# Four graph layers on one core: 64-column products in blocks of 24, a price for fp32 weight loads in the planner, a row's wide product last, and a second strip buffer

## The chip, the core and the metric

The kernel runs on one core of a Trainium2 chip. The engines that matter here are TensorE (PE in the profile; its weight loads are listed apart as PEld), VectorE (DVE), ScalarE (ACT), GpSimd (POOL) and SyncE (SP), which issues nearly all DMAs. The metric is device time in microseconds, the median over the runs; lower is better.

## The reference

There are 16 independent graphs of 1024 nodes with 128 features. Each graph has an adjacency matrix of 1024 x 1024 floats, of which some 1.5% are not zero and whose pattern is symmetric. Four layers follow each other. Each takes h = relu(layernorm(x)) and adds its result to x:

```
layer 0   z = adj^T h / degree ; relu([h, z] W^T + b)
layer 1   leaky_relu((adj h / degree) W^T + b)
layer 2   twice: s[n, m] = sigmoid(relu(a[n] + b[m] + be1) . we2 + be2), a = x Wa, b = x Wb
                 messages = (adj * s) x ; two dense products on [x, messages] ; layernorm
layer 3   e = leaky(wh1[n] + wh2[m]) on the edges ; softmax over m ; attention times Wh ; elu
```

Layer 2 is the costly one. The score s needs a 128-wide hidden vector for every pair of nodes, and only pairs with an edge matter.

## The kernel before

**Edges instead of pairs.** The nodes of a graph are cut into 8 tiles of 128. A bucket is a pair of tiles (t, u); there are 28 off the diagonal and 8 on it. `count` and `build` find, for every bucket, the edges in it and make one-hot fp8 matrices: `st` and `om` bring node features to edge slots (up to 320 slots off the diagonal, 480 on it), `onT` and `omT` bring scores from slots back to a 128 x 128 block. Buckets are handled in 9 groups of four: a diagonal group, seven groups off the diagonal, a diagonal group.

**A round** (`round`, one for each of the two sublayers of layer 2) walks over the 9 groups. For each bucket and direction, `gather` makes a row `pre` in PSUM: two products with `om` moving (320 or 480 columns, L1345) and two with `st` moving (176 or 240 columns, L1351), all added into one bank. The stationary operands are the node features: their fp16 high and low parts, `parts` and a copy of them with swapped halves, `both`, which a DMA makes. ACT (L1366) and DVE (L1367) turn the row into two fp16 parts of `hid`. `dots` multiplies `hid` by a sign column in products of one column each (L1391), ACT applies tanh (L1412), and `scores` spreads the scores with one DVE multiplication of 1024 elements for each direction (`val`, L1443). `scatter` (L1488) adds them into a bank `p`, of which there is one: the first direction with full 128-column output, the second direction (d = 1) with products that write 64 of the 128 output partitions each, 6 for a bucket and 24 for a group. These are the rows `128*64` in the profile, called 64-column products here after the columns of the array that they use. DVE then multiplies the bank by the adjacency block (`upd`, L1495), and `messages` (L441) multiplies by the features in fp32.

**Three lanes.** `weave` generates the work of three lanes side by side: `main` of batch b (lane m, the two rounds), `last` of batch b-1 (lane c: the second update of layer 2 and layer 3) and `first` and `build` of batch b+1 (lane a: layers 0 and 1, then the one-hot matrices). Lanes a and c consist mostly of fp32 products. Layer 3 in lane c walks over strips of the transposed adjacency: a strip is fetched by a DMA on SP's queue (L1579), three DVE operations and one ACT operation work on it (`e`, L767 to L773), and PE multiplies (`hp`, L441). The strips lie in a tile with the tag `strip`, which has one buffer. Layer normalization (`spread`) puts its statistics into a tile `bn`, which has two.

**The planned order.** The order in which the lanes were generated isn't the order of issue. When all operations are recorded, `Issue` lists them with the engine, an estimated duration (`costs`) and the tiles that they use, and plans one order for each engine's queue. `walk` goes through the operations in the order of time: on each queue it takes, of those that are ready, the one with the highest rank. Ranks come from a walk backward from the end; `order` repeats this in four passes and keeps the plan that ends first; `settle` ties the operations of each engine into the planned order, SP's DMA issues included. On PE the walk adds a price when one product follows another of a different form, and the form is narrow or not:

```python
    def switched(self, j, was, back):
        one, two = (self.form[j], was) if back else (was, self.form[j])
        return 0.0 if one == two else NARROW_NS if two else WIDE_NS
```

with 94 ns into the narrow form and 119 ns out of it. The estimated duration of a narrow product is 29 ns, of other fp16 or fp8 products n / 2.4 + 2.5 ns, and an fp32 product counts two passes of at least 112 ns. Nothing is added for a weight load that the product before it is too short to hide. The 24 narrow products of a group are 24 separate entries for the planner.

Of the kernel before, what the change touches and what calls it, by code (L numbers as in the profile page):

```python
# [10 lines left out]
F32 = mybir.dt.float32  # L11
# [48 lines left out]
RESULT_NS = {"PE": 163.0, "Activation": 120.0, "DVE": 88.0, "Pool": 80.0}  # L60
NARROW_NS, WIDE_NS, HELD_NS = 94.0, 119.0, 130.0
DMA_NS, DMA_NS_PER_BYTE, DMA_NS_BEHIND, DMAS = 1900.0, 3.9e-3, 3.3e-3, 8
PASSES = 4


class Issue:
# [3 lines left out]
    def __init__(self, tc, ops, fixed):  # L70
        self.tc, self.ops, self.fixed = tc, ops, fixed
        self.tiles = {t.name: t for t in tc.tiles}
        self.queue = [str(i.engine).split(".")[-1] for i in ops]
        self.kind = [type(i).__name__.removeprefix("Inst") for i in ops]
        self.links()
        self.costs()

    def span(self, arg):
# [51 lines left out]
    def costs(self):  # L130
# [3 lines left out]
        for op, queue, kind in zip(self.ops, self.queue, self.kind):  # L134
            out, form = op.outs[0].bass_ap, False
# [3 lines left out]
            if kind == "Matmult":  # L139
                n = self.size(op.ins[0])  # L140
                form = out.shape[0] < 128
                if op.ins[0].dtype == F32:
                    busy = max(n / 1.2 + 6, 112) * (1 if op.is_transpose else 2)
                else:
                    busy = 29 if form else max(n / 2.4 + 2.5, 25)
            elif kind == "DMACopy":
                size = n * WIDTH[op.outs[0].dtype] * out.shape[0]
                inside = all(a.space == bass.MemoryType.SB for a in (out, aps[0]))
                busy = 630 if inside else 470
                late = DMA_NS + size * DMA_NS_PER_BYTE - busy  # L150
            elif queue == "Activation":
                busy = n / 1.2 + (50 if psum else 92) + 92 * (len(aps) - 1)
            elif queue == "DVE":
                wide = [a for a in aps if a.size() > 128]
                fast = kind == "TensorScalarPtr" and len(wide) == 1 and not psum
                if kind in ("BNStats", "TensorReduce"):
                    n = self.size(op.ins[0])
                busy = n * (0.53 if fast else 1.0625) + 55 + 64 * (len(aps) - len(wide))
                rows = {v[1] for v in map(self.span, (*op.ins[:1], *op.outs[:1])) if v}
                busy += HELD_NS * (len(rows) > 1)  # L160
            else:
                busy = 1560
            self.bytes.append(size)
            self.busy.append(busy)
            self.late.append(busy + late)
            self.form.append(form)

    def joined(self):
# [23 lines left out]
    def switched(self, j, was, back):  # L192
        one, two = (self.form[j], was) if back else (was, self.form[j])
        return 0.0 if one == two else NARROW_NS if two else WIDE_NS

    def walk(self, rank, seq, back=False):
# [8 lines left out]
        soon, now = {q: [] for q in queues}, {q: [] for q in queues}  # L205
        free, sent, was = dict.fromkeys(queues, 0.0), [(0.0, 0.0, 0)] * DMAS, False

# [22 lines left out]
        for _ in range(n):  # L230
# [4 lines left out]
            while soon[q] and soon[q][0][0] <= at:  # L235
                heappush(now[q], heappop(soon[q])[1:])
            j = heappop(now[q])[1]
            more = 0.0
# [6 lines left out]
            elif q == "PE":  # L245
                at += self.switched(j, was, back)
                was = self.form[j]
            start[j], free[q] = at, at + self.busy[j]
# [52 lines left out]
def tile_four_gnn_layers(  # L301
# [142 lines left out]
    class Layers:  # L444
# [22 lines left out]
        def small(self, shape, tag, name):  # L467
            return self.work.tile(shape, F32, tag=f"{tag}{self.lane}", name=name)

# [329 lines left out]
    class Edges:  # L799
# [115 lines left out]
        def scale_terms(self):  # L915
# [15 lines left out]
            for l in range(L):  # L931
                for h in range(2):
# [3 lines left out]
                    )  # L936
            bnd = work.tile([P, L], F32, tag="end", name="bnd")
            nc.vector.tensor_reduce(
# [47 lines left out]
        def strip(self, name):  # L986

            if self.rows_of.get("c"):
                return flat(self.row("c", name))
            return self.work.tile([P, 2 * 3 * P], F32, tag="strip", name=name, bufs=1)  # L990

# [79 lines left out]
        def count(self, s, has, name):  # L1071
# [12 lines left out]
            s.wid = self.work.tile([P, nb], F32, tag="wid", name=f"wid_{name}")  # L1084
            end = self.work.tile([P, nb], F32, tag="end", name=f"end_{name}")
            nc.vector.tensor_scalar(s.wid, s.cnt, -1.0, None, op0=OP.add)
# [203 lines left out]
        class Group:  # L1290
# [43 lines left out]
            def gather(self, i):  # L1334
# [5 lines left out]
                for d in range(self.nd):  # L1340
                    pre = path.m.one(f"pre_{self.name}_{i}_{d}")

                    parts, _ = path.parts[u // Q]
                    for k in range(2):
                        nc.tensor.matmul(  # L1345
                            pre[:, :c], parts[:, k, u % Q, 1 - d], om,
                            start=(k == 0), stop=True, skip_group_check=True,
                        )
                    _, both = path.parts[t // Q]
                    for k, (at, first) in enumerate(((0, 0), (c - n, back))):  # L1350
                        ins = nc.tensor.matmul(  # L1351
                            pre[:, at : at + n], both[:, k, t % Q, d], st[:, first : first + n],
                            start=False, stop=True, skip_group_check=True,
                        )
# [462 lines left out]
```

## Time and profile before

| | |
|---|---|
| median of 3 runs | 4661.11 us (4647.63 to 4667.04) |
| profiled execution | 4639.45 us, span 4637.7 us |
| granted TensorE clock, mean | 0.982 |
| PE | 4359.0 us, 94% of the span, 53685 products |
| weight loads (PEld) | 3581.9 us, 77% |
| DVE | 3873.0 us, 84% |
| ACT | 2992.3 us, 65% |
| POOL | 194.4 us, 4% |
| DMA | 603.41 MB, 130 GB/s on average |

The span runs from the first to the last instruction of one profiled execution. An fp32 product of the program appears as two passes in the records. Busy time of PE counts a product from its start to its end, and products overlap, so a row of the timeline such as `0.86 ... x24` gives the time from the first start to the last end of 24 products. The distance from one row's start to the next row's start tells how long PE needed. In the timeline a name such as `p<-omT,val` means the tile that is written and the tiles that are read, and `128*64 128x128` means 128 rows and 64 columns of the array with 128 elements moving for each partition. A batch takes some 280 to 290 us.

### The profile page before, as it was taken

The page shows a single profiled execution, that of the slowest core. Times are in us where ns is not written, and L with a number is a line of the kernel's source. Part 1 is how long each engine was busy: PE and PEld are TensorE (multiplying, and loading weights), DVE is VectorE, ACT ScalarE, POOL GpSimd, SP SyncE. Part 2 cuts the span into 40 slices and gives each one's busy share as a digit, 9 for nine tenths or more (in the row PEclk, how much of TensorE's full clock was granted, in tenths as well). Part 3 has the DMA queues.
Part 4 walks back from the last instruction along what each step waited for, and adds up shares of the span by engine and source line. Part 5 has one row for each costly group of instructions (what it writes and reads, how often), then busy time and mean ns, then how long its engine had stood idle before and what let it go on. Part 6 is the DMA issues. An engine that isn't in the chain of part 4 may idle for free.

```text
span 4637.7 us, 132212 instructions
## 1 busy us (share of the span) xinstructions
PE 4359.0 (94%) x53685; PEld 3581.9 (77%) x53685; DVE 3873.0 (84%) x9128; ACT 2992.3 (65%) x7238; POOL 194.4 (4%) x137
## 2 busy tenths in 40 slices
PE   6999999999999999999999999999999999999986
PEld 5787778777787777878878787777877777788765
DVE  4777797987979889797897979879797897979977
ACT  5666575675756767576675766757576675766643
POOL 0000100000000000000000000000000000000000
PEclk7999999999999999999999999999999999999997
DMA  7262635445363542635436353453634436344221
GB/s 213 66 198 68 196 94 164 114 127 162 90 185 100 147 142 83 196 107 147 126 94 198 89 162 115 130 165 85 189 103 140 142 83 196 107 145 123 80 80 57
DMA packets 852857, 603.41 MB, mean 130 GB/s; under 512 B 128528, under 2 KB 782608, under 8 KB 852240
## 3 DMA queue, kind: packets, MB, share of 16 engines
q1 hardware_dynamic: 847136, 593.24, 44.3%
q8 instruction: 423, 6.93, 0.6%
q10 hardware_dynamic: 5104, 1.65, 0.1%
q14 instruction: 194, 1.59, 0.1%
HBM read 446.44 MB, written 100.66 MB: 118 GB/s over the span
## 4 chain that ended last, share of the span: by engine, by line
PE 63%; DVE 21%; ACT 6%; DMA 6%; issue 2%; SPq 1%; POOL 1%; ACTq 0%; DVEq 0%; POOLq 0%
PE pre L1345 8%; PE nb L545 8%; PE p L1488 7%; PE msg L441 7%; PE sc L1391 5%; PE pre L1351 5%; DVE hid L1367 4%; PE h L599 4%; DVE val L1443 3%; PE hp L441 3%; PE bb L553 2%; PE xn L608 2%; PE tn L1040 2%; DMA at<-in_adj_dram 2%; DMA both<-part 2%
## 5 line engine op out<-in xcount | busy, mean ns | idle before, releaser
L1367 DVE SCALAR_TENSOR_TENSOR hid<-pre,hid 128x320 f16<-128x320 f32 (+1 forms) x2048 | 1004.1, 508 | 168.6 <-ACT hid L1366 157.9
L1366 ACT ACTIVATE hid<-pre 128x320 f16<-128x320 f32 (+1 forms) x2048 | 906.0, 461 | 330.0 <-PE pre L1351 301.4
L1345 PE MATMUL pre<-om,part 128*128 128x320 fp8e4 (+1 forms) x4096 | 970.9, 309 | 9.8 <-DVE hid L1367 3.7
L1351 PE MATMUL pre<-st,both 128*128 128x176 fp8e4 (+1 forms) x4096 | 681.5, 244 | 21.9 <-DMA both<-part 21.5
L1443 DVE TENSOR_TENSOR val<-onT,u 128x1024 f32<-128x1024 fp8e4 x576 | 695.5, 1218 | 1.6
L441 PE MATMUL msg<-upd,xf 128*128 128x128 f32 (+3 forms) x3008 | 638.7, 327 | 3.8 <-DVE upd L1495 3.8
L1351 PEld LDWEIGHTS <-both 128*128 128x128 f16 x4096 | 392.6, 98 | 180.1 <-issue 35.9
L1391 PE MATMUL sc<-slide,hid 128*128 128x1 f16 x12800 | 435.4, 163 | 28.5 <-DVE hid L1367 26.4
L1391 PEld LDWEIGHTS <-hid 128*128 128x128 f16 x12800 | 410.0, 96 | 53.4 <-DVE hid L1367 40.9
L441 PEld LDWEIGHTS msg<-upd,xf 128*128 128x128 f32 x3008 | 414.4, 191 | 27.6 <-DVE upd L1495 5.5
L1412 ACT ACTIVATE tan<-sc,be_s,down 128x8 f32<-128x8 f32 (+1 forms) x960 | 296.6, 358 | 193.8 <-PE sc L1391 189.1
L1495 DVE SCALAR_TENSOR_TENSOR upd<-p,adj 128x512 f32<-128x512 f32 x512 | 351.6, 687 | 72.4 <-PE p L1488 70.5
L1206 ACT ACTIVATE om<-pm 128x320 fp8e4<-128x320 f32 (+1 forms) x576 | 270.4, 469 | 206.7 <-PE pm L1152 200.0
L1488 PE MATMUL p<-val,omT 128*128 128x64 f16 (+1 forms) x6528 | 373.0, 204 | 27.9 <-DVE val L1443 26.9
L1345 PEld LDWEIGHTS <-part 128*128 128x128 f16 x4096 | 345.2, 98 | 69.0 <-issue 36.8
L1488 PEld LDWEIGHTS <-omT 128*128 128x128 fp8e4 x6528 | 329.3, 97 | 55.0 <-issue 45.4
L441 PE MATMUL hp<-wh,e 128*128 128x129 f32 x2048 | 328.7, 287 | 16.7 <-DVE e L773 16.6
L1191 ACT ACTIVATE onT<-pn 128x256 fp8e4<-128x256 f32 (+1 forms) x576 | 252.3, 438 | 68.1 <-PE pn L1137 62.5
L441 PEld LDWEIGHTS hp<-wh,e 128*128 128x128 f32 x2048 | 274.3, 195 | 26.8 <-DVE e L773 21.7
L1116 DVE TENSOR_SCALAR st<-far,wid 128x384 fp8e4<-128x384 f16 (+1 forms) x576 | 238.6, 428 | 59.4 <-PE pre L1351 37.8
L1112 ACT ACTIVATE far<-iota_off,mid 128x384 f16<-128x384 f16 x448 | 270.0, 625 | 17.3 <-DVE st L1116 14.7
L545 PEld LDWEIGHTS nb<-z,l 128*128 128x128 f32 x2048 | 254.8, 194 | 33.8 <-issue 19.3
(224 smaller groups left out, 7890.8 us busy)
## 6 DMA issues: line engine op xcount, KB each, us to landing
at<-in_adj_dram SPq DMA_DIRECT2D x128, 512.0 KB, 5.1
ct<-in_adj_dram SPq DMA_DIRECT2D x128, 512.0 KB, 5.4
adjT<-tn SPq DMA_DIRECT2D x128, 512.0 KB, 6.3
l<-adjT SPq DMA_DIRECT2D x128, 512.0 KB, 5.8
adj<-adjT SPq DMA_DIRECT2D x256, 256.0 KB, 3.5
a<-adjT SPq DMA_DIRECT2D x128, 384.0 KB, 3.8
both<-part SPq DMA_DIRECT2D x256, 128.0 KB, 3.4
adj<-adjT SPq DMA_DIRECT2D x448, 64.0 KB, 2.6
```

Source lines behind the costliest of these rows:

```text
L441: nc.tensor.matmul(dst, left, right, start=opened is None, stop=True, skip_group_check=True)
L545: nc.tensor.matmul(ps, mat[:, k], z[:, k], start=(k == 0), stop=(k == T - 1))
L1206: nc.scalar.activation(om, pm, AF.Copy, saturate=False)
L1345: nc.tensor.matmul(pre[:, :c], parts[:, k, u % Q, 1 - d], om, start=(k == 0), stop=True, skip_group_check=True,)
L1351: ins = nc.tensor.matmul(pre[:, at : at + n], both[:, k, t % Q, d], st[:, first : first + n], start=False, stop=True, skip_group_check=True,)
L1366: nc.scalar.activation(hid[:, 0, :c], pre[:, :c], AF.Relu)
L1367: nc.vector.scalar_tensor_tensor(hid[:, 1, :c], pre[:, :c], 0.0, hid[:, 0, :c], op0=OP.max, op1=OP.subtract)
L1391: nc.tensor.matmul(sc[:, k, g : g + 1], self.hid[self.done + g][:, v, at : at + P], sign, start=(g, v, k) == (*order[0], 0), stop=True, sk ...
L1412: nc.scalar.activation(dst, src, AF.Tanh, bias=path.be2[:, self.l : self.l + 1], scale=path.down[:, self.l : self.l + 1],)
L1443: nc.vector.tensor_tensor(val, onT[:, i : i + each].rearrange("p i (c n) -> p i c n", n=n), v.rearrange("p k i o -> p i k o").to_broadcast ...
L1488: nc.tensor.matmul(dst, left, right, start=n < first, stop=True, skip_group_check=True)
L1495: nc.vector.scalar_tensor_tensor(upd, ps, S_SCALE, self.adj[:, d * Q : (d + 1) * Q], op0=OP.add, op1=OP.mult,)
```

## The change

The planner gets four things. Products have one of three forms instead of two: narrow, full, and wide for fp32 ones. `switched` adds to the price of a change of form a price for an fp32 load behind a product of another form: what is missing from 108 ns in the duration of the product ahead. `blocks` finds runs of narrow products that write the same tile (the bank `p`), moves the needs of all of them to the first, and so makes one block of the 24. And `walk`, once PE is inside a block, goes on with that block as long as members of it are ready.

In `gather` the order of the four products of a row becomes `om`, `st`, `st`, `om`; only the first opens the accumulation, as before.

The strip of layer 3 gets two buffers instead of one. The tiles `bn`, `seen`, `end` and `bnd` get one buffer instead of two.

```diff
-NARROW_NS, WIDE_NS, HELD_NS = 94.0, 119.0, 130.0
+NARROW_NS, WIDE_NS, LOAD_NS, HELD_NS = 94.0, 119.0, 108.0, 130.0
...
             if kind == "Matmult":
                 n = self.size(op.ins[0])
-                form = out.shape[0] < 128
+                form = "narrow" if out.shape[0] < 128 else "full"
                 if op.ins[0].dtype == F32:
+                    form = "wide"
+
                     busy = max(n / 1.2 + 6, 112) * (1 if op.is_transpose else 2)
                 else:
-                    busy = 29 if form else max(n / 2.4 + 2.5, 25)
+                    busy = 29 if form == "narrow" else max(n / 2.4 + 2.5, 25)
...
+    def blocks(self):
+
+
+        line = [j for j in range(len(self.ops)) if self.queue[j] == "PE"]
+        self.block, run = {}, []
+        for j in (*line, None):
+            if j is not None and self.form[j] == "narrow" and (
+                not run or self.uses[j][-1] == self.uses[run[0]][-1]
+            ):
+                run.append(j)
+                continue
+            for k in run:
+                self.block[k] = run[0]
+                if k > run[0]:
+                    for i, done in self.needs[k].items():
+                        if i not in run:
+                            self.needs[run[0]][i] = self.needs[run[0]].get(i, False) or done
+            run = [j] if j is not None and self.form[j] == "narrow" else []
...
     def switched(self, j, was, back):
-        one, two = (self.form[j], was) if back else (was, self.form[j])
-        return 0.0 if one == two else NARROW_NS if two else WIDE_NS
+        if was is None:
+            return 0.0
+        k, i = (j, was) if back else (was, j)
+        one, two = self.form[k], self.form[i]
+        if one == two:
+            return 0.0
+        cost = NARROW_NS * (two == "narrow") + WIDE_NS * (one == "narrow")
+        return cost + max(0.0, LOAD_NS - self.busy[k]) * (two == "wide")
...
-            j = heappop(now[q])[1]
+            if q == "PE" and len(now[q]) > 1 and was in self.block:
+                best = min(now[q], key=lambda v: (self.block.get(v[1]) != self.block[was], v))
+                now[q].remove(best)
+                heapify(now[q])
+                j = best[1]
+            else:
+                j = heappop(now[q])[1]
...
                 at += self.switched(j, was, back)
-                was = self.form[j]
+                was = j
...
         def small(self, shape, tag, name):
-            return self.work.tile(shape, F32, tag=f"{tag}{self.lane}", name=name)
+            more = {"bufs": 1} if tag in ("bn", "seen") else {}
+            return self.work.tile(shape, F32, tag=f"{tag}{self.lane}", name=name, **more)
...
-            return self.work.tile([P, 2 * 3 * P], F32, tag="strip", name=name, bufs=1)
+            return self.work.tile([P, 2 * 3 * P], F32, tag="strip", name=name, bufs=2)
...
-            end = self.work.tile([P, nb], F32, tag="end", name=f"end_{name}")
+            end = self.work.tile([P, nb], F32, tag="end", name=f"end_{name}", bufs=1)
...
                     parts, _ = path.parts[u // Q]
-                    for k in range(2):
+                    _, both = path.parts[t // Q]
+                    terms = [
+                        (pre[:, at : at + n], both[:, k, t % Q, d], st[:, first : first + n])
+                        for k, (at, first) in enumerate(((0, 0), (c - n, back)))
+                    ]
+                    ends = [(pre[:, :c], parts[:, k, u % Q, 1 - d], om) for k in range(2)]
+                    for k, (dst, left, right) in enumerate((ends[0], *terms, ends[1])):
                         nc.tensor.matmul(
-                            pre[:, :c], parts[:, k, u % Q, 1 - d], om,
-                            start=(k == 0), stop=True, skip_group_check=True,
-                        )
-                    _, both = path.parts[t // Q]
-                    for k, (at, first) in enumerate(((0, 0), (c - n, back))):
-                        ins = nc.tensor.matmul(
-                            pre[:, at : at + n], both[:, k, t % Q, d], st[:, first : first + n],
-                            start=False, stop=True, skip_group_check=True,
+                            dst, left, right, start=k == 0, stop=True, skip_group_check=True
                         )
```

## The prediction

> **What bounds the kernel now.** I read the page's engine rows first, then the span cut into stretches of 24 us, then single products in the timeline.
>
> ```profile
> span 4637.7 us, 132212 instructions
> PE 4359.0 (94%) x53685; PEld 3581.9 (77%) x53685; DVE 3873.0 (84%) x9128; ACT 2992.3 (65%) x7238; POOL 194.4 (4%) x137
> PE   6999999999999999999999999999999999999986
> DVE  4777797987979889797897979879797897979977
> ```
>
> PE has the highest share, but its matmuls overlap in these records, so the 94% doesn't say how much PE work is needed. For that I take distances from one start to the next. With nothing to wait for they are 25 ns after a 1-column product, 56 after 128 columns, 76 after 176, 135 after 320, 112 after a pass of an fp32 128-column product, and 28 on average inside a row of 64-column products. Summed over the trace's 53685 products this is 3966 us; what is found below for changes of form adds 112 us and for exposed weight loads 94 us. So 4172 of 4625 us (90%) are PE work and some 450 are waits, 140 of them in the first 200 and the last 240 us. PE is the bound on the whole. Not everywhere, though: the stretches (columns are length, then busy time of PE, PEld, DVE, ACT, POOL) show DVE full for part of each batch.
>
> ```profile
> 2024.00:2048.00 24.00, 23.12 (x380) 19.40 (x379) 23.88 (x51) 18.24 (x50) 0.00 (x0) 1.00 0.27 74
> 2168.00:2192.00 24.00, 24.00 (x298) 20.78 (x296) 14.25 (x36) 12.28 (x26) 0.00 (x0) 1.00 0.96 287
> 2288.00:2312.00 24.00, 23.11 (x359) 19.61 (x357) 23.84 (x49) 16.97 (x45) 0.00 (x0) 1.00 0.28 79
> ```
>
> At 2024 and 2288 DVE has 0.1 to 0.2 us to spare in 24; at 2168 it is idle for 10 and PE has no gap. Of the 176 such stretches between 216 and 4440 us, counted through, 51 show DVE busy for 23.5 us or more. PE time saved there helps only if DVE's work moves elsewhere.
>
> **What a change of form costs.** One stretch of PE's timeline (start us, us, instruction):
>
> ```profile
> 2313.28 0.29 PE L1137 MATMUL pn<-eye,st 128*128 128x64 f16 x3
> 2313.50 0.75 PE L1488 MATMUL p<-omT,val 128*64 128x128 fp8e4 x20
> 2314.18 0.34 PE L1195 MATMUL pq<-rank,st 128*128 128x128 f16 x3
> 2314.45 0.25 PE L1488 MATMUL p<-omT,val 128*64 128x128 fp8e4 x2
> 2314.63 0.31 PE L1345 MATMUL pre<-om,part 128*128 128x320 fp8e4 x1
> ```
>
> The three pq products need 3 x 56 = 168 ns, but the p products start 270 ns after them: going into the 64-column form costs about 94 ns over the whole trace. Twenty p products need 560 ns and the next work starts 680 later: coming out costs about 121. The two p products at the end (56 ns) cost 0.18 us. One such interruption costs 0.215 us. The trace holds 521.
>
> **What an fp32 weight load costs.** The same two passes of a 129- or 128-column fp32 product, after different products:
>
> ```profile
> 1943.68 0.37 PE L1345 MATMUL pre<-om,part 128*128 128x480 fp8e4 x1
> 1943.88 0.39 PE L441 MATMUL hp<-wh,e 128*128 128x129 f32 x2
> ...
> 2032.32 0.31 PE L1351 MATMUL pre<-st,both 128*128 128x176 fp8e4 x2
> 2032.47 0.42 PE L441 MATMUL hp<-wh,e 128*128 128x129 f32 x2
> ...
> 2004.68 0.30 PE L1152 MATMUL pm<-eye,omT 128*128 128x128 f16 x3
> 2004.82 0.47 PE L441 MATMUL hp<-wh,e 128*128 128x129 f32 x2
> ...
> 4361.74 0.53 PE L1488 MATMUL p<-omT,val 128*64 128x128 fp8e4 x12
> 4362.19 0.49 PE L441 MATMUL msg<-upd,xf 128*128 128x128 f32 x2
> ```
>
> 0.39 after a wide product, 0.42 after 176 columns, 0.47 after 64 columns, 0.49 after a 64-wide block. The load is some 108 ns, hidden to the length of the product before it: 0, 33, 80 and 101 ns stay.
>
> Here a rule speaks against the change. The Trainium skill, "TensorE: Matmul & The Clock Gate", "The mechanism", says that "LDWEIGHTS overlaps with in-flight MATMULs only when row_grp differs". All these loads fill all rows, so by the rule none is hidden, the order in front of an fp32 product doesn't matter, and the load part below is 0. The rows of 0.39 and 0.47 are the same product and differ by what stands ahead, so I take the rows.
>
> **The change part by part**, counted in the instruction order that each kernel builds, up to the test of the flag.
>
> *Blocks of 24.* The 64-column products (scatter, L1488, second direction) stood in runs of 1 to 24; now all stand in 224 blocks of 24 (7 groups x 2 rounds x 16 batches). Interruptions fall from 521 to 224: 297 x 0.215 = 64 us of PE time.
>
> *Wide product last, and a price for loads.* fp32 products behind a 176-column one fall from 748 to 37 (711 x 33 ns = 23.5 us), behind a 64-wide block from 208 to 61 (147 x 101 = 14.8); those behind 64-column full products rise from 186 to 260 (74 x 79 = 5.8 lost), and the others nearly cancel. Net 33 us. The products and the sum of the row are the same, so its `hid` (L1366, L1367) isn't later by this; `both` is needed one product (135 ns) earlier, against 21.5 us in all that PE waits for it now.
>
> Together PE has 97 us less to do. Which part shortens the span? In the 51 stretches with DVE full lie 204 of 521 interruptions and 30 of the 94 us of loads, so about 25 + 10 = 35 us of the saving; 62 lie where PE has no gap. Of those I count nine tenths (56), since PE's gaps there are also ended by ACT and DVE. Of the 35 I count from nothing (DVE is full) to all (the planner shifts DVE work into its idle stretches), and take 12. Sum 68.
>
> *Second strip buffer, single buffers.* SP waits 144.2 us for `e` L773 (53 times) before it may issue the next strip, with `st` and `adj` copies behind it in its queue. DVE itself waits for strips only 7.8 + 3.9 us, and where DVE is full. The gain lies between 0 and these 11.7 us, plus what of the copies behind comes earlier; I take 5. The strip issues that follow each other at once rise from 12 to 36; one may then stand ahead of an `st` copy (0.37 us of issue), against copies that land 2.6 to 6.7 us after issue: below 1 us, taken as 0. Single `bn`, `end`, `seen`: all are written and read on DVE within one short chain, so the next use waits for nothing but DVE's own order. If that fails, 128 chains x 0.17 us (L499) = 22 us of DVE; I take 0.
>
> *The new order.* A block occupies PE for 24 x 28 = 0.67 us and nothing may go between. A `pre` row ready behind it comes on average 0.34 us later, and ACT and DVE with it. Runs were partly long already, so I take 3 us for all; the bounds are 0 and 224 x 0.34 = 76. The order of all queues is planned afresh; nothing in the trace prices that, some 10 us either way.
>
> Net 68 + 5 - 3 = 70 us. The profiled execution took 4639.45 us (span 4637.7 and 1.75 around it); the median of the three runs, 4661.11, is 0.47% above it. So 4569 for a profiled run and 4591 for the median, 1.5% less.
>
> **Rivals.**
> *DVE takes over.* DVE is full in 51 of the 176 stretches, and above 23.0 us in 56. If the stretches that are full grow as PE gets faster, only a third of the 97 us comes out: about 4630. For: the strip buffer lets layer 3 run earlier, into or out of these stretches. Against: DVE has 760 us idle in all.
> *All of it comes out.* 97 + 11.7 = 109 us: 4552. For: over the middle of the span PE's gaps are only some 7%.
> *Blocks starve DVE.* The same block that saves PE time stands ahead of `pre` rows and DVE, full now, gets holes. Now DVE waits 70.5 us for p (L1495) and ACT 301.4 us for pre. It decides from 0.33 us per block (73 / 224); with the whole 0.67 us lost at each, 150 us are lost against 73 won: 4738. With half of the blocks hurt, the result is no change. Against: the products of a block share one `val`, so they are ready together, and `upd` gets the p bank complete sooner.
> *No effect as built* is excluded by the counts of the order; loads that cost the same in any order (the rule above) would leave 64 us of PE time, about 42 on the path: 4619.
>
> **How the numbers follow.** A measurement of this kernel tells about 0.5% (23 us) from no change; three runs spread over 19 us. Likeliest case (half to all of the 70, smaller loads included): 0.55. All of it: 0.17. DVE takes over, 4615 to 4660: 0.20, a third of it beyond the 0.5% bound. Starved: 0.08. Faster 0.55 + 0.17 + 0.06 = 0.78, same 0.14, slower 0.08. The range goes from 4540 (all of it, and a low run) to 4658 (nothing gained); about 1 in 10 is left above and below.
>
> **What would show it.** Right: in the new profile PE's L1488 64-column rows read x24 throughout; after `pre<-om` the two fp32 passes take 0.39, not 0.42; PE busy falls by 60 to 100 us at 53685 instructions, DVE stays near 3870, and its share rises to about 85%. SP's wait on L773 falls from 144 us to below 50. Wrong: more stretches with DVE at 23.5 of 24 us and PE gaps ended by DVE growing (DVE takes over); ACT's waits for `pre` well above 301 us or DVE's for p above 70 (starved); passes at 0.42 or more after wide products (the load price).

## The result and the profile after

| | before | after |
|---|---|---|
| median | 4660.0 us (4647.63 to 4667.04, 4 runs) | 4624.06 us (4621.3 to 4627.59, 4 runs) |
| profiled execution, span | 4637.7 us | 4622.3 us |
| granted TensorE clock, mean | 0.982 | 0.973 |
| 64-column runs | 521 | 224 |

The ratio is 0.9926, with a 95% interval of 0.9904 to 0.9948; measured once more later, 0.9929 (0.991 to 0.9948). So the change brings 0.7%, some 34 us, where 1.5% (70 us) was forecast. Lines have new numbers: `pre` L1345/L1351 is L1387, `p` L1488 is L1523, `hid` L1366/L1367 is L1401/L1402, `upd` L1495 is L1530, `e` L767/L773 is L803/L809, the fp32 helper L441 is L476.

The page of after, span, engine rows and the two slices:

```profile
span 4622.3 us, 132151 instructions
PE 4338.9 (94%) x53685; PEld 3592.5 (78%) x53685; DVE 3855.7 (83%) x9128; ACT 3004.6 (65%) x7238; POOL 193.6 (4%) x137
PE   6999999999999999999999999999999999999986
DVE  4787797897979889698896978979798896988986
```

PE still shows 94%. Its busy time fell by 20 us, not by the 60 to 100 foretold, and DVE's share is 83%, not 85: products overlap in these records, so less time between two starts need not show as less busy time. Both things that the change was to do are there. In after's timeline of PE the 64-column products stand 24 in a row, and an fp32 product behind a wide product (here an `om` of 480 columns) reads 0.39:

```profile
2112.70 0.86 PE L1523 MATMUL p<-omT,val 128*64 128x128 fp8e4 x24
2122.56 0.86 PE L1523 MATMUL p<-omT,val 128*64 128x128 fp8e4 x24
...
2180.41 0.86 PE L1523 MATMUL p<-omT,val 128*64 128x128 fp8e4 x24
2181.20 0.49 PE L476 MATMUL msg<-upd,xf 128*128 128x128 f32 x2
...
2210.45 0.57 PE L1387 MATMUL pre<-om,part 128*128 128x480 fp8e4 x2
2210.86 0.39 PE L476 MATMUL hp<-wh,e 128*128 128x129 f32 x2
```

From 2180.41 to 2181.20 are 0.79 us: 24 x 28 ns and the 121 ns for coming out. The prices hold in the new order.

The same account as in the prediction (distances from start to start over all products) shows where the saving went. The four sums, worked out from the two traces (one execution each):

| us | before | after |
|---|---|---|
| products alone | 3966 | 3966 |
| changes of form | 112 | 48 |
| exposed fp32 loads | 94 | 64 |
| the rest: waits, and products at half clock | 453 | 531 |

The 94 us of PE work are gone as computed, and 78 us came back in the last row. These 78 need two remarks. The profiled execution of before was faster than all four of its runs in the table above, so the two executions differ by 15 us and the medians by 36; an estimated 20 of the 78 us belong to that one execution. And some 35 of them are not waits. The granted clock of TensorE is 1 or 0.5 in these records. Away from the first 200 and the last 240 us it was 0.5 for 44 us before and for 133 us after (130 in c1, the same kernel measured once more), and products take twice as long there: those that ran at half clock in the whole trace, 57 us of work at full clock before and 101 after, took some 46 and 81 us longer than that. One stretch of 24 us in each trace, first before, then after (length, then busy time of PE, PEld, DVE, ACT, POOL, granted clock, DMA share, GB/s):

```profile
2232.00:2256.00 24.00, 21.61 (x205) 16.78 (x204) 22.11 (x62) 13.75 (x31) 2.64 (x2) 0.93 0.30 98
2232.00:2256.00 24.00, 19.26 (x236) 15.81 (x236) 21.61 (x56) 14.64 (x41) 2.57 (x2) 0.86 0.31 93
```

By what ended them, waits for DVE grew from 174 to 225 us, the part with no recorded releaser (mostly products at half clock) from 65 to 97, those for ACT from 141 to 147; those for DMAs fell from 60 to 46. Rows of PE's waits (us in total, times, the longest), first before, then after:

```profile
PE p L1488 <- DVE val L1443: 26.9, 42, 1.9
PE sc L1391 <- DVE hid L1367: 26.4, 40, 1.4
```

```profile
PE tp L1571 <- DVE xf L663: 42.5, 14, 3.2
...
PE hp L476 <- DVE e L809: 18.1, 18, 3.9
PE sc L1426 <- DVE hid L1402: 17.8, 37, 1.5
PE p L1523 <- DVE val L1478: 13.9, 28, 1.4
```

One new wait, 14 times and 3 us on average, stands at the top: `tp` is the transposing of the features behind the layer norm between the two rounds. Before, the same product waited 1.7 us in all. In after's timeline of one batch:

```profile
2232.99 0.68 DVE L523 BATCH_NORM_STATS2 bn<-x 128x6 f32<-128x128 f32 x3
2233.57 1.11 DVE L657 TENSOR_SCALAR xf<-xf,st_y 128x128 f32<-128x128 f32 x4
2234.58 0.31 DVE L523 BATCH_NORM_STATS2 bn<-x 128x6 f32<-128x128 f32 x1
2234.78 0.70 DVE L662 TENSOR_TENSOR xf<-xf,gamma_bc 128x512 f32<-128x512 f32 x1
2235.38 0.31 DVE L523 BATCH_NORM_STATS2 bn<-x 128x6 f32<-128x128 f32 x1
2235.58 0.70 DVE L663 TENSOR_TENSOR xf<-xf,beta_bc 128x512 f32<-128x512 f32 x1
2236.17 0.51 DVE L523 BATCH_NORM_STATS2 bn<-x 128x6 f32<-128x128 f32 x2
2236.33 0.95 PE L1571 MATMUL tp<-ident,xf 128*128 128x128 f32 x4 [3.07 <-DVE xf L663]
```

DVE is busy without a gap, partly with another lane's layer norm (`bn<-x`), and the next product in PE's order is `tp`, so PE stands until `xf` is scaled.

Two more stretches of 24 us of after, in the same columns:

```profile
2016.00:2040.00 24.00, 23.17 (x385) 19.81 (x383) 23.76 (x52) 19.01 (x53) 0.00 (x0) 1.00 0.27 75
2160.00:2184.00 24.00, 24.00 (x196) 18.69 (x195) 14.80 (x32) 15.45 (x27) 0.00 (x0) 1.00 0.89 273
```

The pattern is that of before. Of 176 stretches DVE has 23.5 us or more in 46 (51 before), 23.0 or more in 67 (56 before).

### The profile page after: what moved, and what is told of

Same layout as the page of the kernel before. It is cut to its first block, busy times and chain, and to the rows that moved or that the text cites. A ratio compares the mean times of both kernels' runs of the same rounds, so it can differ in the third digit from the quotient of the medians.

```text
span 4622.3 us, 132151 instructions
## 1 busy us (share of the span) xinstructions
PE 4338.9 (94%) x53685; PEld 3592.5 (78%) x53685; DVE 3855.7 (83%) x9128; ACT 3004.6 (65%) x7238; POOL 193.6 (4%) x137
## 4 chain that ended last, share of the span: by engine, by line
PE 48%; DVE 37%; DMA 6%; ACT 5%; issue 3%; POOL 1%; SPq 1%; DVEq 0%; ACTq 0%; POOLq 0%
PE pre L1387 10%; DVE hid L1402 8%; PE nb L581 7%; PE p L1523 5%; DVE val L1478 5%; PE msg L476 4%; PE h L635 4%; PE sc L1426 3%; DVE upd L1530 3%; DVE omT L1235 3%; DVE e L803 3%; PE bb L589 2%; DVE e L807 2%; PE tn L1076 2%; DVE e L809 2%
## 5 line engine op out<-in xcount | busy, mean ns | idle before, releaser
L1387 PE MATMUL pre<-om,part 128*128 128x320 fp8e4 (+1 forms) x4096 | 1161.1, 310 | 25.2 <-DVE hid L1402 11.8
L1401 ACT ACTIVATE hid<-pre 128x320 f16<-128x320 f32 (+1 forms) x2048 | 915.4, 461 | 342.5 <-PE pre L1387 331.9
L1402 DVE SCALAR_TENSOR_TENSOR hid<-pre,hid 128x320 f16<-128x320 f32 (+1 forms) x2048 | 1002.4, 508 | 101.9 <-ACT hid L1401 93.0
L1387 PE MATMUL pre<-st,both 128*128 128x176 fp8e4 (+1 forms) x4096 | 682.1, 244 | 8.4 <-DMA both<-part 8.2
L476 PE MATMUL msg<-upd,xf 128*128 128x128 f32 (+3 forms) x3008 | 626.7, 323 | 8.7 <-DVE upd L1530 8.7
L1387 PEld LDWEIGHTS <-both 128*128 128x128 f16 x4096 | 390.6, 98 | 163.1 <-issue 52.9
L476 PEld LDWEIGHTS msg<-upd,xf 128*128 128x128 f32 x3008 | 424.8, 192 | 24.4 <-DVE upd L1530 11.2
L1523 PE MATMUL p<-val,omT 128*128 128x64 f16 (+1 forms) x6528 | 399.4, 206 | 14.9 <-DVE val L1478 13.9
L1387 PEld LDWEIGHTS <-part 128*128 128x128 f16 x4096 | 392.7, 99 | 19.4 <-issue 5.6
L1523 PEld LDWEIGHTS <-omT 128*128 128x128 fp8e4 x6528 | 351.9, 98 | 50.1 <-issue 26.8
L1530 DVE SCALAR_TENSOR_TENSOR upd<-p,adj 128x512 f32<-128x512 f32 x512 | 351.9, 687 | 19.0 <-PE p L1523 13.0
L476 PE MATMUL hp<-wh,e 128*128 128x129 f32 x2048 | 322.4, 286 | 18.7 <-DVE e L809 18.1
L476 PEld LDWEIGHTS hp<-wh,e 128*128 128x128 f32 x2048 | 277.0, 195 | 28.0 <-DVE e L809 22.5
```

The lines of the kernel that those rows point to most:

```text
L476: nc.tensor.matmul(dst, left, right, start=opened is None, stop=True, skip_group_check=True)
L1387: nc.tensor.matmul(dst, left, right, start=k == 0, stop=True, skip_group_check=True)
L1401: nc.scalar.activation(hid[:, 0, :c], pre[:, :c], AF.Relu)
L1402: nc.vector.scalar_tensor_tensor(hid[:, 1, :c], pre[:, :c], 0.0, hid[:, 0, :c], op0=OP.max, op1=OP.subtract)
L1523: nc.tensor.matmul(dst, left, right, start=n < first, stop=True, skip_group_check=True)
L1530: nc.vector.scalar_tensor_tensor(upd, ps, S_SCALE, self.adj[:, d * Q : (d + 1) * Q], op0=OP.add, op1=OP.mult,)
```

## Experiments

The figures are medians and the ratio to the kernel before, with its 95% interval; a difference to after is the difference of the ratios times 4650 us. After has 0.9926 and 0.9929 (0.9928 in what follows), so such a difference is uncertain by some 11 us.

### Parts of the change in the order of before

These keep the planned order of before and move only products of PE. Theories A and B, named with e1, both expect a gain or nothing from every one of them.

**e1, blocks.** The 64-column products of a bank go to the place of the last of them.

```diff
-        for line in self.order().values():
+        lines = self.order()
+        lines["PE"] = self.together(lines["PE"])
+        for line in lines.values():
```

> The order planned for the kernel before is kept on every queue; alone the 64-column products of a bank are moved together, to the place of the last of them. Interruptions fall from 521 to 224, PE's priced work by 71 us (switches 64, loads 7), with nothing planned anew. Theory A (the PE time saved comes back as waits, because DVE's queue and the chain at the start of a round set the pace of a batch): 0 to -25 us. Theory B (PE time is worth its share, and the newly planned order is what lost it): two thirds arrive, about -45 us.

Measured: 4681.65 us, ratio 1.0061 (1.0045 to 1.0077). Interruptions fell from 521 to 224 and 71 us of PE's priced work went, and the kernel is 28 us slower, which neither theory allowed. PE's waits of before and of e1 (its lines stand 22 further down):

```profile
PE pq L1195 <- ACT onT L1191: 13.1, 20, 0.8
PE pn L1137 <- ACT om L1206: 11.1, 23, 0.7
```

```profile
PE pq L1217 <- ACT onT L1213: 34.7, 64, 0.8
...
PE pn L1159 <- ACT om L1228: 22.7, 47, 0.7
```

PE's waits ended by ACT rose from 141 to 225 us in all. The rows say that the split runs had been fillers: the planner put a few 64-column products where PE would otherwise have waited for the next one-hot matrix, so that much of their 0.215 us had been paid out of idle time.

**e2, the wide product last.** In the four planned places of a row stand `om`, `st`, `st`, `om`.

```diff
+            for n, k in zip(at, (0, 2, 3, 1)):
+                out[n] = r[k]
```

> The order planned for the kernel before is kept on every queue, but in the four places of each row the products stand as om, st, st, om. fp32 loads behind 176-column products fall from 748 to 94; 21 us less exposed load. Theory A: 0 to -7 us. Theory B: about -14 us. If a load is not hidden by the wide product after all: 0, with fp32 pairs still at 0.42 us.

Measured: 4830.03 us, 1.0379 (1.0364 to 1.0394): 176 us slower, for 21 us fewer loads. PE's first row of waits:

```profile
PE pre L1375 <- DMA both<-part: 188.5, 46, 9.4
```

It was 21.5 us before. The prediction took `both` to be needed one product (135 ns) earlier. In the first group of a round that is wrong, as before's timeline of a second round shows (its first `om` and its first `st`):

```profile
2217.92 0.38 PE L1345 MATMUL pre<-om,part 128*128 128x480 fp8e4 x1
...
2229.33 0.47 PE L1351 MATMUL pre<-st,both 128*128 128x240 fp8e4 x3 [1.92 <-DMA both<-part]
```

In these 11.4 us stand six `om` and some fifty passes of other lanes' fp32 products, and they gave the copy that makes `both` most of its time. With the planned places kept, `st` comes ahead of much of this work. After's own plan waits only 8.2 us for `both`.

**e4, both.**

```diff
+        lines["PE"] = self.together(self.swapped(lines["PE"]))
```

> Both moves of the two kernels before this one on the order planned for the kernel before, which is otherwise kept: 94 us less PE work (the changed kernel has 97 less). One strip buffer. Theory A: -10 to -40 us, no better than the changed kernel's own -34. Theory B: about -60 us, clearly better than the changed kernel.

Measured: 4855.21 us, 1.0422 (1.0406 to 1.0438). Within the intervals the two losses add up (0.6% and 3.8%).

**e5, the wide product last except in the first group of each round,** so that the copy keeps its time.

```diff
+                if name.startswith("pre_") and name.split("_")[3] != "0":
```

> The order planned for the kernel before, kept on every queue; rows have the wide product last except in the first group of each round, where the features' copy is still on its way. Priced PE work falls by 21 us (748 fp32 loads behind 176 columns become 96 behind 240 or fewer). The first try had +12 us a batch at those first groups and nothing gained elsewhere. If PE time is worth nothing in a fixed order: 0 to -3 us. If it is worth two thirds: -14 us.

Measured: 4657.25 us, 1.0014 (1.0002 to 1.0026). PE waits 34.5 us for `both`, 13 more than before, which leaves 8 of the 21 us of PE work to gain; the time shows none of it, and rather a loss of 1 to 12 us.

### Parts taken back from after

**e3** keeps after's order and puts `om`, `om`, `st`, `st` into a row's places.

```diff
+            for n, k in zip(at, (0, 3, 1, 2)):
+                out[n] = r[k]
```

> The changed kernel with its planned order kept on every queue, but the four products of each row in the old order om, om, st, st: 21 us of exposed loads come back. Theory A: 0 to +7 us against the changed kernel (4624). Theory B: +14 us against it.

Measured: 4661.63 us, 1.001 (1.0002 to 1.0019), 38 us more than after for 21 us of loads. A loss of 2.8 us a batch, as large as all of it, arises at the second round's first groups, where no load changed. So it isn't the price of the loads. In one batch these rows stand there, first of after, then of e3 (its lines stand 24 further down):

```profile
2226.26 1.73 PE L581 MATMUL nb<-z,l 128*128 128x128 f32 x14
```

```profile
2246.26 0.49 PE L605 MATMUL nb<-z,l 128*128 128x128 f32 x2 [1.38 <-DVE o L646]
...
2247.72 3.02 PE L605 MATMUL nb<-z,l 128*128 128x128 f32 x14
```

A new wait for DVE is 1.4 us of it, and the same 14 passes take 1.3 us longer (mean granted clock 0.72 from 2246 to 2252 us, 1.00 in after at that place). Why the row order brings that wait was not looked into.

**f1** has the old row order, **f2** no blocks, **f3** one strip and two of the small tiles; each is planned afresh. The edits, shortened:

```diff
f1  -  ends[0], *terms, ends[1]     +  *ends, *terms
f2  -  self.blocks()                +  self.block = {}
f3  -  tag="strip", bufs=2          +  tag="strip", bufs=1    (bn, seen, end: 2)
```

> The changed kernel with the old order om, om, st, st in a row, planned anew. PE has 17 us more exposed loads by the count of the order (82.5 against 65.2). If the row order carries the gain: about 4660, no better than before. If PE's work counts two thirds: +12 us, 4636. If re-planning alone decides: anything within some 15 us of 4624.

> The changed kernel whose planner makes no blocks (prices, row order and strips as changed), planned anew: 377 interruptions instead of 224, priced PE work 44 us more. If interruptions are paid in full: +30 us (4654). If they fill holes that PE would have anyway, as the kernel with blocks moved together in the old plan showed: 0 to -15 us (4610 to 4624).

> The changed kernel with one strip buffer and two of bn, seen and end, planned anew. My prediction gave the strips 5 us: 4629. If the second strip is what lets layer 3 run early: +15 us or more. If the single bn holds up the norms: faster than 4624.

Measured: f1 4653.09 us, 1.0001 (0.9988 to 1.0013); f2 4699.62 us, 1.0099 (1.0083 to 1.0116); f3 4659.44 us, 1.0015 (1.0002 to 1.0028). Against after 34, 80 and 41 us slower. Taken as prices of the parts these would sum to 155 us, four times what the change brings.

**f4 and b4** tell what such numbers are worth: after and before with every price of the planner raised by 1 ns, a change of nothing but the plan. **c1** is after once more, measured beside them.

```diff
-NARROW_NS, WIDE_NS, LOAD_NS, HELD_NS = 94.0, 119.0, 108.0, 130.0
+NARROW_NS, WIDE_NS, LOAD_NS, HELD_NS = 95.0, 120.0, 109.0, 130.0
```

> The changed kernel with prices one ns higher in the planner alone (95, 120 and 109 for 94, 119 and 108). The chip does the same work; by the count of the order PE's priced work is 117 us against 113. Whatever it differs from the changed kernel is scatter of the plan. If the plan is stable: within 5 us. If the plan's scatter is as large as the effect of the change: 10 us or more, either way.

> The kernel before with prices one ns higher in the planner alone (95 and 120 for 94 and 119): 504 interruptions for 521, priced PE work 209 us for 210. If the plan is stable: within 5 us of the kernel before. If its scatter is as large as the change's effect: 10 us or more, either way.

> The changed kernel itself, on the same chip as the three kernels beside it, so that they have a measure: 0.9926 of the kernel before, as measured first.

Measured: f4 4636.22 us, 0.9969 (0.9961 to 0.9977); b4 4682.4 us, 1.0072 (1.0051 to 1.0094); c1 4617.14 us, 0.9929 (0.991 to 0.9948). The same work in a slightly other plan costs 19 us more for after and 33 us more for before. Two things follow. A single replanned variant can't price a part within 30 us, so f1 and f3 decide nothing and f2 little. And after was faster than before at both settings (34 us, and 0.9969 against 1.0072, 48 us), so the gain is not luck of one plan alone. But two settings do not say how large it is on average, and both kernels of this text are the faster of their two plans.

### What sets the pace

**h1** tests whether DVE's order makes the hole at `tp`: in after's DVE order the steps of the layer norm between the rounds go ahead of what stood between them.

```diff
+        lines["DVE"] = self.hoisted(lines["DVE"])
```

> The changed kernel and its planned order, except on DVE: in the layer norm of a half between the two rounds, what the plan has put between the steps of the chain (up to the variance, and from the first scaling to the last addition) goes behind them. No work is added or removed. The trace of the changed kernel has a hole of 3 to 5 us on PE there once in a batch, ended by the last addition. Theory C (this chain is where the saved PE time waits): 2 to 3.5 us a batch less, -30 to -50 us against the changed kernel (4624). Theory A' (DVE's total work sets the pace): 0, since DVE does the same work. Theory D (another chain waits as long): 0 to -10 us.

Measured: 4647.14 us, 0.9993 (0.9982 to 1.0005), 30 us slower than after, which none of its theories allowed. Waits at the start of the second round, products at half clock included, stayed at 8.1 us a batch (7.7 in after), so this other order on DVE does not close the hole; at half clock, away from the first 200 and the last 240 us, are 167 us (133 in after). The guess that what was moved behind is missing elsewhere was not followed up.

The last six runs keep a planned order instruction for instruction and take nearly the same amount of work from different places, so their results are no longer the reference's. g1 and g2 apply gamma and beta to 1 of each 128 columns in one of the two layer norms, g3 takes 150 of the 176 columns of a product with `st` moving, and the planner is given the old durations. g1 to g4 start from after; the line for beta is changed as the one for gamma:

```diff
g1, g2 (l = 0: between the rounds; l = 1: lane c)
+            part = slice(0, 1) if l == 0 else slice(0, D)
-            nc.vector.tensor_mul(dst, dst, over_t(rows["gamma"][:, l], Q))
+            nc.vector.tensor_mul(dst[:, :, part], dst[:, :, part], over_t(rows["gamma"][:, l], Q)[:, :, part])
...
g3
+                    cut = n - 26 if n == 176 else n
-                        (pre[:, at : at + n], both[:, k, t % Q, d], st[:, first : first + n])
+                        (pre[:, at : at + cut], both[:, k, t % Q, d], st[:, first : first + cut])
```

> The changed kernel with the same planned order; the scaling by gamma and the adding of beta in the layer norm between the two rounds (lane up, L662 and L663 on xf) take 1 of each 128 columns instead of all, so 64 DVE operations of 0.69 us become some 0.13 us: 36 us less DVE work, all of it in the chain from the end of a round to the start of the next, whose hole (7.7 us a batch) it shortens by 1.1 us in each half. If the chain at the round's start sets the time: 18 us (one half of it on the path, 16 x 1.1) to 36 us less than the changed kernel. If it does not: 0 to 8. If DVE's load as such sets the pace: as much as the kernel with less DVE work in lane c.

> The changed kernel with the same planned order; the same two operations in the layer norm of the second update (lane c, L662 and L663 on y) take 1 of each 128 columns: the same 36 us less DVE work, but in a lane on whose result nothing in the same batch's rounds waits. If DVE sets the pace in the stretches where it is busy for 95% and more: 25 to 36 us less. If PE does, and DVE's work lies beside it: 0 to 8 us.

> The changed kernel with the same planned order; each product with st moving off the diagonal takes 150 columns instead of 176 (26 slots at one end of each row get only part of their sum), 3584 products x 10.8 ns = 39 us less PE work, spread over all the rows. Prediction's step (PE is the bound wherever it has no gap, nine tenths arrive): 30 us or more less than the changed kernel. If waits take it back as in the change itself (15 to 35 of 94 us came out): 6 to 15 us. If DVE alone sets the pace: 0.

> The three cuts together (72 us of DVE work, 39 us of PE work), same planned order. If they are independent: the sum of the three gains. If PE and DVE bound each other (a gain on one is a wait on the other until both have less): clearly more than the sum of the three. If the pace is set in one place only: no more than the largest of the three.

b1 and b3 are the cuts of g1 and g3 in before and its order.

> The kernel before, its planned order kept, with the same 36 us of DVE work left out of the layer norm between the rounds (gamma and beta on 1 of each 128 columns). In the new order that cut was worth about 26 us. If the chain between the rounds set the pace before as well: 20 to 30 us faster than before. If PE set the pace before and the chain became the bound only through the change: 0 to 12 us.

> The kernel before, its planned order kept, with 150 instead of 176 columns in each product with st moving off the diagonal: 39 us less PE work, of which 748 loads behind the shorter products take 8 back, so 31 us. The prediction's own step (PE is the bound where it has no gap, nine tenths of what lies there arrive): 20 us or more faster than before. If a given order hides PE savings in its waits, as it did in the new order (0 of 39) and with e5 (0 of 21): 0 to 6 us.

| work taken away | in after's order | in before's order |
|---|---|---|
| 35 us of DVE, between the rounds | g1 4588.48 us, 0.9872 (0.985 to 0.9893): 26 us | b1 4631.2 us, 0.9962 (0.995 to 0.9974): 18 us |
| 35 us of DVE, lane c | g2 4606.06 us, 0.9908 (0.9891 to 0.9925): 9 us | |
| 39 us of PE (31 net in before) | g3 4612.57 us, 0.993 (0.9913 to 0.9946): -1 us | b3 4634.43 us, 0.9978 (0.997 to 0.9986): 10 us |
| all three | g4 4580.24 us, 0.9856 (0.9835 to 0.9877): 33 us | |

The gains in after's order are against after, uncertain by some 11 us; those in before's order are against before, uncertain by 6 (b1) and 4 us (b3). The spans of the single profiled executions fall by more: 31.7 for g1, 15.3 for g2, 15.6 for g3, 40.5 for g4.

The groups of g1 (its lines stand 3 further down; us busy, mean ns, and idle time ahead with its releaser) show the cut, first the two operations, then the transposing that waits for them:

```profile
L665 DVE TENSOR_TENSOR xf<-xf,gamma_bc 128x4 f32<-128x4 f32 x32 | 4.9, 152 | 0.0
L666 DVE TENSOR_TENSOR xf<-xf,beta_bc 128x4 f32<-128x4 f32 x32 | 4.9, 152 | 0.0
...
L1574 PE MATMUL tp<-ident,xf 128*128 128x128 f32 x128 | 25.1, 329 | 26.9 <-DVE xf L666 26.9
```

152 ns instead of 691 is 64 x 0.54 = 35 us. PE's wait at `tp` falls from 42.5 to 26.9 us, 15.6 us or about half of the cut, as it would if only one of a batch's two halves stood in PE's way. A microsecond of DVE in that chain is worth some 0.7 (0.4 to 1.1 with the error), in lane c about a quarter (from nothing to 0.6), and on PE nothing that these runs can tell from zero (0.4 by the span of its one profile). By the medians the three cuts together give the sum of the three, 33 against 34 us, and show no second bound behind the first; by the spans of one profile each they give less, 40.5 against 62.6, so this is not settled.

In g3 the account of PE's time shows how a saving on PE gets lost: 39 us less of products, and waits for DVE up from 225 to 247 us, for ACT from 147 to 153. Time at half clock hardly changed there.

## Why half of the predicted gain came

**Changes of form: the size was right.** 521 interruptions became 224, as counted. At the 0.215 us each that the traces show, that is 64 us.

**Loads: the size was right.** 0.39 us behind the wide product, 0.49 behind a block; from 94 to 64 us, 30 where 33 were expected. The weighing of the rule against the row was right as well: the order in front of an fp32 product does matter to PE.

**What of it arrives: this step failed.** The prediction counted 62 of the 97 us as lying "where PE has no gap", nine tenths of them as gain, and 12 of the other 35: 68 in all. By the ratio 34 us arrived, by the two traces 15. In place of the rest stand 51 us more of waits ended by DVE and some 35 us more of products at half clock.

The first error is the nine tenths. That PE has no gap in a stretch doesn't say that a saving in it arrives. PE's waits are many and short: of the 453 us before, some two thirds are in pieces below 1 us, and in batches 3 to 12 they make, with products at half clock, 20 of a batch's 281.4 us. The 120 us from 110 ahead of a batch's first `tp` between the rounds to 10 behind it hold only 1.8 of these 20. There the priced work (changes of form and loads) fell by 2.7 of the 5.7 us that PE saves in a batch, and the waits rose to 5.2: the saving left even where PE had hardly waited. (After's plan puts partly other work there.) In before's own order b3 prices PE work with the clock unchanged at 0.980: 10 us (6 to 14) of 31 arrive, a third, where the prediction's 68 of 97 are seven tenths. With a third of 97 the sum would have been 32 + 5 - 3 = 34 us, which is what was measured; but e1 gave a loss and e5 nothing in the same order, so that agreement is luck.

The second error is a term that the prediction put at nothing, without a word: the granted clock. It went from 0.982 to 0.973 in the profiled executions. In the 43 runs of before that were measured beside c1, a run whose mean clock was lower by 0.001 took some 4 us longer (in other such series 3.2 to 3.8); after's 0.973 against their 0.980 would by this be some 25 to 30 us. That is an estimate from a correlation. It agrees with the 35 us of the traces, but no run changed the clock alone.

**The rival that came closest** is "DVE takes over", which said "only a third of the 97 us comes out: about 4630". Its sign was half there: the waits of PE that DVE ended grew by 51 us, but the stretches with DVE at 23.5 us or more went down from 51 to 46, while those at 23.0 or more went up from 56 to 67. One chain on DVE counted for more than DVE's load: g1 is worth three times g2 for the same load, 26 against 9 us, though their errors of 11 us each leave the factor loose. The chain wasn't made by the change; b1 shows 18 us (12 to 24) for it in before's order, between its two forecasts, though the row of `tp` showed only 1.7 us of waiting there. The same lateness must have lain in other waits; which ones was not traced.

**"All of it"** fell, and **"blocks starve DVE"** too: DVE's wait for the bank fell from 70.5 to 13.0 us (the block is complete sooner), ACT's wait for `pre` rose from 301 to 332 us, and the time fell.

**Strips.** DVE's two waits for a strip's DMA, 7.8 and 3.9 us, became 0.3 and 6.2: 5 us less in all, the amount taken in the sum. SP's wait did not fall as foretold (144 to below 50): it is 155.5 us, presumably since SP, with a buffer more, issues further ahead and then waits for the next one. What the strips are worth in time stays open, since f3 cannot tell.

**Moving the wide product costs nothing: right only for a new plan.** e2 shows 176 us where the planner can't answer. The small wait that the prediction relied on (21.5 us in all) was the work of the plan, which had put other products ahead of the first `st`.

**The plan.** "Some 10 us either way" was too small: f4 and b4 give 19 and 33.

What stays open: how much of the 34 us is PE work that arrived and how much is a better plan, and how much the clock took. In fixed orders PE work removed gave a loss (e1), nothing clear of the error (e5, g3) or a third (b3); the gain came only with planning afresh. What is better in after's plan is not known.

## What to carry to other kernels

A busy share of 94% says that an engine is nearly always at work, not that a microsecond less on it is a microsecond gained: take some known amount of work away in a fixed order, from each engine in turn, and count what arrives, before costing a change by its work. Before calling what is missing a wait, compare the granted clock of the two traces. Where a planner fills waits with work that has a price, removing the price first removes the filler. Where a plan is computed afresh, run the same kernel under two or three plans that differ by a nanosecond before reading a variant's difference as the price of its edit.

## What the runs showed of the hardware

The hole at `tp` comes with a second cost: at each of the 14, TensorE's granted clock goes to half within 3 us of the hole's end. The stretches of after around that place (columns as above, the clock after POOL):

```profile
2231.00:2237.00 6.00, 2.22 (x16) 1.48 (x15) 6.00 (x21) 1.46 (x4) 1.01 (x1) 0.96 0.23 92
2237.00:2242.00 5.00, 4.87 (x46) 3.90 (x45) 3.80 (x10) 1.80 (x4) 0.00 (x0) 0.50 0.16 56
```

PE had been busy for 2.2 of 6 us, and the next 5 us run at 0.50. A pair of products ahead of the hole and behind it:

```profile
2232.54 0.43 PE L1387 MATMUL pre<-om,part 128*128 128x320 fp8e4 x2
...
2241.65 0.74 PE L1387 MATMUL pre<-om,part 128*128 128x320 fp8e4 x2
```

The mean granted clock of 0.973 over 4622 us means some 250 us at half clock, 0.982 over 4638 us some 167 us before. At 4.87 us of PE work in 5 us at half clock, the place costs an estimated 2 to 3 us more than the wait itself. That the length of this wait brings the clock down is not shown. In g1's trace it is mostly 2.0 us instead of 3.1, and half clock still stands beside 13 of the 14: away from the first 200 and the last 240 us it lasts 126 us against 133. Before has no such hole and still 13 stretches of 3.4 us at half clock in that part; ahead of 12 of them the longest single wait within 14 us was below 1.5 us. So thin work around a wait may count as well as its length; no run tried them apart.
